# Row maxima of a causal attention kernel: diagonal pairs first, with half of their masking moved to ScalarE and GpSimd

## The chip, the cores and the metric

The kernel runs on one core of a Trainium2 chip. The metric is the device time of one execution in microseconds. Of the five engines four compute: TensorE (PE in the profile; its weight loads are PEld), VectorE (DVE), ScalarE (ACT) and GpSimd (POOL). SyncE (SP) issues most DMAs. Each engine takes its own instructions in the order in which the program lists them, and waits on semaphores for the others.

## What is computed

One transformer block in float32 on 4096 tokens of 256 features: causal attention with 16 heads of 16 features, and then a feed-forward network. Only the attention matters here.

```python
h = layernorm(x)
q, k, v = split(h @ w_attn + b_attn)            # 16 heads of 16 features
logits = einsum('bhqd,bhkd->bhqk', q, k) * hd ** -0.5
logits = where(causal, logits, -inf)
weights = softmax(logits, axis=-1)
out = einsum('bhqk,bhkd->bhqd', weights, v) @ w_proj + b_proj
x = x + layernorm(out)
...                                              # the feed-forward network
```

The softmax needs the maximum of each row of the logits (one query, one head, all keys up to the query). The kernel computes all logits twice: once with queries on the partitions, to find the maxima, and once with keys on the partitions, to take the exponential and to multiply by v.

## The kernel before

**Tiling.** Queries come in 8 blocks j of 512, heads in 4 groups g of four. An *item* is one (j, g); there are 32, worked off in the order of j, then g. Keys come in chunks c of 512, and because the attention is causal block j needs the chunks 0 to j. Tiles of 128 queries in a block are t = 0 to 3.

**Steps.** Item (j, g) has 4(j+1) steps kt, each of 128 keys. In a step the loop at line 946 does, in the order of the program:
- the first half of a *pair* of the maxima (`MaxUnit`, lines 612 to 687): the logits of 128 queries against one chunk of 512 keys, for heads 2 and 3 of the group (`pr` is 1), two matmuls into two PSUM banks of the three-bank pool `pm` (L624);
- the scores of this step for heads 0 and 1, then 2 and 3 (`ScoreUnit`, L729): eight matmuls, two of which per bank subtract the row maximum by a product with `ones`; then ScalarE's exponential (L744);
- the second half of the pair (heads 0 and 1, `pr` is 0);
- the values of an earlier step (L779), and pieces of background work: `prep` of the block j+2 (normalization, transposition `pt`, projections `pk`, `pq`, `pv`) and `project` of the block j-1 (`py`), whose GpSimd parts are additions, normalizations and casts.

In the last four steps of an item (kt of 4j to 4j+3) the keys are those of the diagonal chunk. There the scores and values have 512, 384, 256 and 128 columns only, and GpSimd sets the upper triangle of one 128x128 block per head to zero (`affine_select` on e, L749).

**The maxima.** They run ahead of the scores by an item and three pairs (`LEAD`): during item n the loop issues the pairs of item n+1 from its fourth on, and in the last three steps the first three pairs of item n+2. `maxima` (line 600) lists the pairs of an item: for each t the chunks 0 to j, so that each t ends with its diagonal pair, which has (t+1)*128 columns. `MaxUnit.finish` reduces them on VectorE:
- a full pair's head: one `tensor_reduce` of 512 columns (L658). In most steps ScalarE first copies one of the first two heads from PSUM to SBUF (`hold`, L643), and VectorE reduces the copy afterwards (L647); `lent` lists other work of ScalarE that takes this copy's place, and in the last three steps there is none;
- a diagonal pair's head: one masked operation (`tensor_tensor_reduce`, L662) that adds a mask of 0 and -1e30 and takes the maximum, followed by a read of its accumulator;
- after the diagonal pair of t, a small reduction over the chunks into `neg` (L675), and after the last t three small operations that split `neg` into a rounded part and its rest in `mcol` (L681 to L686).

`to_rows` (line 689) turns `mcol` into a row with four matmuls (`pmt`, L694) and a copy on ScalarE (`mrow`, L703), at the end of the next step. The scores of the item need `mrow`.

**What sets the order.** Everything in this part is issued by hand in the order of the loop (`manual_schedule`). The planner is the arithmetic at lines 945 to 952: `due` is the number of pairs of this step. A block's items have as many steps as the next item has pairs, save the last one, whose successor has four more. Up to four extra pairs of a block are issued between the matmuls of the background (`unit_beside`, line 884, in the items g = 0 to 2). The keys of an item come by DMA into a ring of 16 tiles per pair of heads (`keys`, `ask`).

**The start.** `prep` of the blocks 0 and 1 runs first (lines 908 to 915; that of block 1 has its casts on GpSimd), then seven pairs of maxima, then `to_rows` of the first item (lines 916 to 920).

Of the kernel before, what the change touches and what calls it, by code (L numbers as in the profile page):

```python
# [24 lines left out]
LEAD = 3  # L25

# [67 lines left out]
def sandwich_kernel(  # L94
# [131 lines left out]
    for key, at in (("h1", 0), ("h2", FC)):  # L226
        TAGS[key] = {(c, o): f"k{at + c}_{o}" for o in range(2) for c in range(FC)}
# [142 lines left out]
    xT0 = []  # L370


    with ExitStack() as actx:
# [137 lines left out]
        chunks = [(n, c) for n in range(G * NB) for c in range(n // G + 1)]  # L511
        RING = 2 * NB
        kT, asked = {}, [0]

        def keys(n, c):

            for pr in range(2):
                kT[n, c, pr] = load_rows(
                    f"k{asked[0] % RING}_{pr}", f"k{n}_{c}_{pr}", "k", c, 4 * (n % G) + 2 * pr
                )  # L520
            asked[0] += 1

        def ask(n, kt):

            while asked[0] < len(chunks) and chunks[asked[0]][0] <= n + 2:

                if asked[0] >= RING and chunks[asked[0] - RING] >= (n, (kt - 1) // NT):
                    return
                if n >= 2 * G and kt % 2:
                    return  # L530
                keys(*chunks[asked[0]])
                if n >= 2 * G:
                    return
# [66 lines left out]
        def maxima(j, g):  # L600

            mcol = mcols[g % 2]
            neg = stat.tile([P, NT, 4], F32, tag="neg", name=f"neg_{j}_{g}")
            for t in range(NT):
                mx = stat.tile([P, 4, NB], F32, tag="mx", name=f"mx_{j}_{g}_{t}")
                for c in range(j + 1):
                    n = QB if c < j else (t + 1) * P
                    yield [(j, g, t, c, pr, n, mx, neg, mcol) for pr in (1, 0)]  # L610

        class MaxUnit:
            def __init__(self, j, g, t, c, pr, n, mx, neg, mcol):
                self.at = j, g, t, c, pr
                self.n, self.mx, self.neg, self.mcol = n, mx, neg, mcol
                self.ps = {h: bank(f"pm_{j}_{g}_{t}_{c}_{h}") for h in (2 * pr, 2 * pr + 1)}
                self.diagonal = c == j

            def products(self):
                j, g, t, c, pr = self.at  # L620
                n = self.n
                for i, ps in enumerate(self.ps.values()):
                    r = slice(i * P // 2, (i + 1) * P // 2)
                    nc.tensor.matmul(  # L624
                        ps[:, 0:n],
                        lhsT=qT[j, g][pr][r, t * P : (t + 1) * P],
                        rhs=kT[G * j + g, c, pr][r, 0:n],
                        start=True,
                        stop=True,
                    )  # L630

            def finish(self, hold=False):
                j, g, t, c, pr = self.at
                n = self.n
                heads = list(self.ps.items())
                if hold:


                    h, ps = heads.pop(0)
                    held = const.tile(  # L640
                        [P, QB], F32, tag=f"xT0{'hl'[c % 2]}", name=f"held_{j}_{g}_{t}_{c}"
                    )
                    nc.scalar.copy(held[:, 0:n], ps[:, 0:n])  # L643
                    heads.append((h, held))
                for h, ps in heads:
                    if not self.diagonal and hold and ps is held:
                        nc.vector.tensor_scalar(  # L647
                            held[:, 0:n],
                            held[:, 0:n],
                            -3.0e38,  # L650
                            None,
                            ALU.max,
                            ALU.max,
                            accum_out=self.mx[:, h, c : c + 1],
                        )
                        continue
                    if not self.diagonal:
                        nc.vector.tensor_reduce(  # L658
                            self.mx[:, h, c : c + 1], ps[:, 0:n], AX.X, ALU.max
                        )  # L660
                        continue
                    nc.vector.tensor_tensor_reduce(  # L662
                        out=ps[:, 0:n],
                        in0=ps[:, 0:n],
                        in1=mask[:, QB - n : QB],
                        scale=1.0,
                        scalar=-3.0e38,
                        op0=ALU.add,
                        op1=ALU.max,
                        accum_out=self.mx[:, h, c : c + 1],  # L670
                    )
                if not (self.diagonal and pr == 0):
                    return False
                neg, mcol = self.neg, self.mcol
                nc.vector.tensor_reduce(  # L675
                    neg[:, t, :], self.mx[:, :, 0 : j + 1], AX.X, ALU.max, negate=True
                )
                if t < NT - 1:
                    return False
# [3 lines left out]
                col = mcol.rearrange("p t (i pr e) -> p t pr i e", i=2, pr=2)  # L683
# [3 lines left out]
                return True  # L687
# [108 lines left out]
        mcols = [aw.tile([P, NT, P], F32R, tag=f"mcol{i}", name=f"mcol{i}") for i in range(2)]  # L796
        for mcol in mcols:
            nc.gpsimd.memset(mcol.bitcast(F32), 0.0)
# [70 lines left out]

        def issue(unit, **how):  # L870
            unit.products()
            done = unit.finish(**how)
            if done is True:
                rows_due.append((now + 4, unit))
            return done
# [9 lines left out]
        def unit_beside():  # L885
            j, g = item
            if not begun_pair and 1 <= j < NB - 1 and g < G - 1 and len(ahead) < NT:
# [28 lines left out]
        while issued < first[1] + LEAD:  # L916
            for args in next(stream):
                issue(MaxUnit(*args))
            issued += 1
        rows_of(now + 4)  # L920
        for n, (j, g) in enumerate(items):
# [15 lines left out]
            if (j, g) == (NB - 1, G - 1):  # L937
                W["h1"] = weight_pieces("h1", TAGS["h1"])
                load_pieces(rounded["h1"], W["h1"])
            item = j, g  # L940
            if g == G - 1:
                issued += len(ahead)
                ahead.clear()
            begun = issued
            goal = min(first[min(n + 2, len(items))] + LEAD, first[-1])
            for kt in range(count[n]):
# [3 lines left out]
                due = begun + (goal - begun) * (kt + 1) // count[n] - issued  # L950
                pairs = [next(stream) for _ in range(due)]
                issued += due
                es = []
                if pairs:
                    unit = MaxUnit(*pairs[0][0])
                    issue(unit, hold=not (lent or xT0) and unit.n > QB // 2 and kt <= NT * j)
                    lent.clear()
                es = [
                    issue(ScoreUnit(j, g, kt, pr, not pairs and next(alone)))
                    for pr in range(2)  # L960
                ]
                if pairs:
                    issue(MaxUnit(*pairs[0][1]))
                values.step(now + 1)
# [11 lines left out]
                if j > 0 and kt % 4 == 2 and kt < NT * j:  # L976
                    next(halving, None)
            rows_of(now + 2)
# [255 lines left out]
```

## Time and profile before

| What | Value |
|---|---|
| Time, median of 3 runs | 2401.88 us (2397.31 to 2404.38) |
| The profiled execution: time, span | 2401.19 us, 2399.5 us |
| Its mean granted TensorE clock | 0.982 |
| From the start to the first steps (0 to 80 us) | VectorE busy 24.92 us, clock 0.82 |
| Block 0 (80 to 153 us) | VectorE busy 45.81 us of 73, clock 0.78 |
| Blocks 1 to 7 while there are maxima (153 to 1667 us) | PE busy 1484.77, VectorE 1346.93, ScalarE 1246.95, GpSimd 464.84 us of 1514 |
| Last item (1667 to 1736 us) | PE busy 68.68, ScalarE 61.51 us of 69 |
| Feed-forward network (1736 to 2399.5 us) | PE busy 653.57 us of 663.5 |

How to read the profile: times are in microseconds unless marked ns, and L624 is line 624 of the kernel. A group of instructions has its line, engine, operation, output and inputs, count, busy time, mean duration in ns, and the engine's idle time before it with what ended it. A matmul's end is modelled, and its duration is more than its share of the stream, so a busy PE need not be a PE at its peak. The chain of waits is followed back from the last instruction: at each step to what released it, or to the instruction before it on the same engine.

### The profile page before, as it was taken

Reading aid. Unit: us, or ns where it says so; the run is one execution under the profiler, and the core shown is the slowest. Engines: PE = TensorE matmul, PEld = TensorE weight load, DVE = VectorE, ACT = ScalarE, POOL = GpSimd, SP = SyncE. Lnnn points to the kernel's source line nnn. Section 1 sums busy time; section 2 is a strip of 40 time slices with the busy share of each in tenths; the row PEclk is TensorE's granted clock in tenths of the full one; section 3 lists DMA queues with packets and bytes.
Section 4 is the critical chain, followed back from the end, with each engine's and each line's share of the span. In section 5 each row is a group of like instructions: output and inputs, shape, how many; then the busy total and the mean of one; then the engine's idle time right before and its main releaser. Section 6 shows DMA issues by size and latency. Waiting matters only on the chain.

```text
span 2399.5 us, 40893 instructions
## 1 busy us (share of the span) xinstructions
PE 2318.1 (97%) x15237; PEld 1408.6 (59%) x15237; DVE 1768.1 (74%) x4102; ACT 1514.3 (63%) x2087; POOL 565.9 (24%) x898
## 2 busy tenths in 40 slices
PE   4889999999999999999999999999999999999998
PEld 2545554455554555545555555544488888888887
DVE  1667887998999899988999998986056546544653
ACT  1447787887797888888899888976822222222221
POOL 2324334432334223243223321010002100000000
PEclk8879999999999999999999999999999999999999
DMA  4443534433332432244323232111021000000000
GB/s 144 159 151 123 176 101 159 138 115 106 112 97 96 145 123 75 97 159 120 111 77 96 81 115 62 54 54 62 7 97 46 27 1 18 18 18 1 18 9 11
DMA packets 134831, 202.78 MB, mean 85 GB/s; under 512 B 14912, under 2 KB 59584, under 8 KB 134624
## 3 DMA queue, kind: packets, MB, share of 16 engines
q1 hardware_dynamic: 132672, 198.75, 25.4%
q8 instruction: 122, 2.00, 0.4%
q10 hardware_dynamic: 1776, 1.18, 0.2%
q14 instruction: 85, 0.70, 0.1%
q0 software_dynamic: 176, 0.15, 0.1%
HBM read 137.91 MB, written 62.13 MB: 83 GB/s over the span
## 4 chain that ended last, share of the span: by engine, by line
PE 87%; DVE 6%; ACT 2%; DMA 2%; POOL 1%; issue 1%; SPq 0%; ACTq 0%; POOLq 0%; DVEq 0%
PE av L779 21%; PE s L729 19%; PE z L1090 19%; PE pm L624 15%; PE pyf L1172 2%; PE za L1090 2%; PE zb L1090 2%; DVE mx L658 2%; DVE pm L662 2%; PE py L280 1%; PE pk L465 1%; PE pv L586 1%; PE pq L465 1%; PE pmt L694 1%; ACT e L744 1%
## 5 line engine op out<-in xcount | busy, mean ns | idle before, releaser
L744 ACT ACTIVATE e<-s 128x1024 f32<-128x1024 f32 (+3 forms) x1175 | 1039.7, 936 | 101.0 <-PE s L729 90.5
L658 DVE TENSOR_REDUCE mx<-pm 128x1 f32<-128x512 f32 x1496 | 963.1, 685 | 132.1 <-PE pm L624 90.8
L624 PEld LDWEIGHTS pm<-k,q 64*128 64x128 f32 x2304 | 301.2, 186 | 498.6 <-DVE mx L658 344.4
L624 PE MATMUL pm<-k,q 64*128 64x512 f32 (+3 forms) x2304 | 569.8, 439 | 22.8 <-DVE mx L658 11.7
L779 PE MATMUL av<-e,v 128*32 128x512 f32 (+3 forms) x4608 | 580.3, 575 | 0.6 <-POOL e L749 0.6
L729 PE MATMUL s<-q,k 64*128 64x512 f32 (+3 forms) x2304 | 465.2, 389 | 9.6 <-ACT e L744 2.0
L729 PE MATMUL s<-mrow,ones 64*128 64x512 f32 (+3 forms) x2304 | 452.6, 379 | 0.0
L1157 ACT ACTIVATE fb<-z,sh 128x512 f32<-128x512 f32 x128 | 88.3, 690 | 364.8 <-PE z L1090 339.5
L729 PEld LDWEIGHTS s<-q,k 64*128 64x128 f32 x2304 | 230.6, 187 | 79.8 <-issue 17.8
L662 DVE CUSTOM_DVE_ANT_0 pm<-pm,mask 128x128 f32<-128x128 f32 (+3 forms) x463 | 212.6, 499 | 73.1 <-PE pm L624 68.1
L749 POOL TENSOR_SCALAR_AFFINE_SELECT e<-e 128x256 f32<-128x256 f32 x256 | 103.0, 411 | 682.4 <-ACT e L744 680.7
L729 PEld LDWEIGHTS s<-mrow,ones 64*128 64x128 f32 x2304 | 234.3, 187 | 37.1 <-ACT mrow L703 0.5
L643 ACT COPY held<-pm 128x512 f32<-128x512 f32 (+1 forms) x345 | 200.2, 580 | 50.2 <-PE pm L624 17.7
L647 DVE TENSOR_SCALAR_CACHE_REDUCE held<-held 128x512 f32<-128x512 f32 x296 | 200.1, 676 | 0.1
L1090 PE MATMUL z<-hb_0h,h 128*128 128x512 f32 x512 | 199.3, 389 | 0.0
L1090 PE MATMUL z<-hb_0l,h 128*128 128x512 f32 x512 | 199.2, 389 | 0.0
L779 PEld LDWEIGHTS av<-e,v 128*32 128x32 f32 x4608 | 91.6, 108 | 145.5 <-issue 129.0
L202 POOL TENSOR_TENSOR rstd<-ve,neghalf 128x4 f32<-128x4 f32 (+1 forms) x22 | 20.8, 945 | 632.9 <-DVE ve L200 607.4
L1057 DVE CAST hb_1h<-fb 128x512 fp32r<-128x512 f32 x64 | 27.3, 427 | 156.0 <-ACT fb L1157 156.0
L1134 ACT ACTIVATE sl<-za,s 128x512 f32<-128x512 f32 x64 | 44.0, 690 | 120.0 <-PE za L1090 58.2
L1090 PEld LDWEIGHTS z<-hb_0l,h 128*128 128x128 f32 x512 | 96.1, 188 | 19.9
L1090 PEld LDWEIGHTS z<-hb_0h,h 128*128 128x128 f32 x512 | 96.1, 188 | 19.9
(251 smaller groups left out, 2553.6 us busy)
## 6 DMA issues: line engine op xcount, KB each, us to landing
k<-k SPq DMA_DIRECT2D x288, 256.0 KB
q<-q SPq DMA_DIRECT2D x64, 256.0 KB
x<-in_x_dram SPq DMA_DIRECT2D x16, 512.0 KB
k<-hik SPq DMA_DIRECT2D x32, 256.0 KB
k<-lok SPq DMA_DIRECT2D x32, 256.0 KB
q<-hiq SPq DMA_DIRECT2D x32, 256.0 KB
q<-loq SPq DMA_DIRECT2D x32, 256.0 KB
avd<-av_sb SPq DMA_DIRECT2D x32, 256.0 KB
```

The costliest lines, as they stand in the source:

```text
L465: nc.tensor.matmul(ps, lhsT=wqk[d][:, i * D + c * P : i * D + (c + 1) * P], rhs=xTs[j][:, d, :], start=(d == 0), stop=(d == DC - 1),)
L624: nc.tensor.matmul(ps[:, 0:n], lhsT=qT[j, g][pr][r, t * P : (t + 1) * P], rhs=kT[G * j + g, c, pr][r, 0:n], start=True, stop=True,)
L643: nc.scalar.copy(held[:, 0:n], ps[:, 0:n])
L647: nc.vector.tensor_scalar(held[:, 0:n], held[:, 0:n], -3.0e38, None, ALU.max, ALU.max, accum_out=self.mx[:, h, c : c + 1],)
L658: nc.vector.tensor_reduce(self.mx[:, h, c : c + 1], ps[:, 0:n], AX.X, ALU.max)
L662: nc.vector.tensor_tensor_reduce(out=ps[:, 0:n], in0=ps[:, 0:n], in1=mask[:, QB - n : QB], scale=1.0, scalar=-3.0e38, op0=ALU.add, op1=ALU ...
L729: nc.tensor.matmul(self.ps[i][:, self.q0 :], lhsT=(self.k, ones[pr])[m][r, :], rhs=(qT[j, g][pr], mT[j, g])[m][r, self.q0 :], start=(m == ...
L744: nc.scalar.activation(e[:, at : at + n, q0:], ps[:, :, q0:], AF.Exp)
L749: nc.gpsimd.affine_select(out=at, in_=at, compare_op=ALU.is_ge, fill=0.0, base=0, pattern=[[0, 2], [1, P]], channel_multiplier=-1,)
L779: nc.tensor.matmul(self.av[h * HW : (h + 1) * HW, q0:], lhsT=vb[kt // NT][:, kt % NT, o : o + HW], rhs=es[h // 2][:, h % 2, q0:], start=(k ...
L1090: nc.tensor.matmul(ps, lhsT=w[c], rhs=single(part[:, c, :]), start=(c == 0 and i == 0), stop=(c == kc - 1 and i == parts - 1),)
L1157: nc.scalar.activation(h, z, AF.Gelu, scale=sc[:, oc : oc + 1])
```

## The change

- `maxima` lists the four diagonal pairs of an item first, for t = 2, 1, 0, 3, and then the full pairs. With the lead of three pairs, the diagonal pairs t = 2, 1, 0 of item n+2 come in the last three steps of item n, and t = 3 in the first step of the next.
- For heads 2 and 3 of a diagonal pair ScalarE copies the last 128 columns of each head (the block on the diagonal) to SBUF, GpSimd masks the two blocks in one `affine_select`, and VectorE reduces the columns before them with plain reductions (none for t = 0) and the two masked blocks with one reduction, which is put off (`owed`) until `pay`: right after the first half of the pair in the loop, and after both halves in the seven pairs of the start. Heads 0 and 1 keep the masked operation on VectorE.
- The maxima of all t of an item lie in one tile `mx`, with a column more, which GpSimd fills with -1e30 at the item's beginning; one small reduction per item replaces four. It and the operations on `mcol` (now a single tile) are put off in the same way (`end_group`).
- The held copies use fixed tiles (`spares`). The scores' second matmuls come before the second half of the pair and their exponential after it. `to_rows` is due 2 instead of 4 counts of `now` after the (now later) end of the group.
- In blocks 1 to 5 each step has one pair; extra pairs are issued beside the background in the items g = 2 and 3 alone, and what is left in the last step. Block 6 has none beside the background.
- A ring place of the keys comes free when its chunk's scores are done (`homes`, `free`), in the new order of the chunks. The weights h1 and h2 take their tiles accordingly.

```diff
-        chunks = [(n, c) for n in range(G * NB) for c in range(n // G + 1)]
+        chunks = [(n, c) for n in range(G * NB) for c in (n // G, *range(n // G))]
...
+            mx = stat.tile([P, NT, 4, NB + 1], F32, tag="mx", bufs=2, name=f"mx_{j}_{g}")
+            nc.gpsimd.memset(mx[:, :, :, j + 1 : j + 2], NEG)
+            for t in (2, 1, 0, 3):
+                yield [(j, g, t, j, pr, t * P, mx, False) for pr in (1, 0)]
             for t in range(NT):
-                mx = stat.tile([P, 4, NB], F32, tag="mx", name=f"mx_{j}_{g}_{t}")
-                for c in range(j + 1):
-                    n = QB if c < j else (t + 1) * P
-                    yield [(j, g, t, c, pr, n, mx, neg, mcol) for pr in (1, 0)]
+                for c in range(j):
+                    yield [(j, g, t, c, pr, QB, mx, (t, c) == (NT - 1, j - 1)) for pr in (1, 0)]
...
+                if self.diagonal and pr == 1:
+                    edge = spares[t % 2][:, 1, 0 : 2 * P].rearrange("p (h q) -> p h q", h=2)
+                    if len(owed) > 1:
+                        owed.popleft()()
+                    for i in range(2):
+                        nc.scalar.copy(edge[:, i, :], self.ps[i][:, n : n + P])
+                    if n:
+                        for i in range(2):
+                            nc.vector.tensor_reduce(
+                                self.mx[:, t, 2 + i, j + 1 : j + 2], self.ps[i][:, 0:n], AX.X, ALU.max)
+                    nc.gpsimd.affine_select(
+                        out=edge, in_=edge, compare_op=ALU.is_ge, fill=NEG,
+                        base=0, pattern=[[0, 2], [-1, P]], channel_multiplier=1)
+                    owed.append(
+                        lambda: nc.vector.tensor_reduce(self.mx[:, t, 2:4, j], edge, AX.X, ALU.max))
+                    return
...
-            if not begun_pair and 1 <= j < NB - 1 and g < G - 1 and len(ahead) < NT:
+            if not begun_pair and 1 <= j < NB - 2 and g >= G - 2 and len(ahead) < NT:
...
+                if 1 <= j < NB - 2:
+                    due = 1
+                    if (g, kt) == (G - 1, count[n] - 1):
+                        due = goal - issued - len(ahead)
...
                     unit = MaxUnit(*pairs[0][0])
-                    issue(unit, hold=not (lent or xT0) and unit.n > QB // 2 and kt <= NT * j)
+                    issue(unit, hold=not (lent or xT0) and kt <= NT * j)
                     lent.clear()
-                es = [
-                    issue(ScoreUnit(j, g, kt, pr, not pairs and next(alone)))
-                    for pr in range(2)
-                ]
+                pay()
+                es = [issue(ScoreUnit(j, g, kt, 0, not pairs and next(alone)))]
+                unit = ScoreUnit(j, g, kt, 1, not pairs and next(alone))
+                unit.products()
                 if pairs:
                     issue(MaxUnit(*pairs[0][1]))
+                es.append(unit.finish())
```

## The prediction

> **What bounds the kernel now.** I read the page's first lines, then its chain of waits, and then the chain and the busy times inside one item. All numbers are of the profiled execution: span 2399.5 us, time 2401.19 us, 0.7 us under the median of 2401.88. A difference below 0.3% (7.2 us) cannot be told from none here.
>
> ```profile
> span 2399.5 us, 40893 instructions
> PE 2318.1 (97%) x15237; PEld 1408.6 (59%) x15237; DVE 1768.1 (74%) x4102; ACT 1514.3 (63%) x2087; POOL 565.9 (24%) x898
> ...
> PE 87%; DVE 6%; ACT 2%; DMA 2%; POOL 1%; issue 1%; SPq 0%; ACTq 0%; POOLq 0%; DVEq 0%
> ```
>
> TensorE carries 87% of the chain and VectorE 6%, about 144 us. Where those 6% lie decides. The chain in order of time inside item (6,1) gives a ruler: each "PE s" starts a step (one kt).
>
> ```profile
> 1197.51 0.93 PE s L729 x8
> ...
> 1200.10 0.93 PE s L729 x8
> ...
> 1202.57 0.92 PE s L729 x8
> ...
> 1205.04 0.93 PE s L729 x8
> ```
>
> An ordinary step takes 2.59 us. In the chain it is TensorE alone: first score pair of the maxima 0.43, scores 0.93, second pair 0.24, values 1.00. The two steps from 1200.10 hold the diagonal pair t=1 (256 columns instead of 512) and take 2.47 each. So **inside an item a diagonal pair is cheaper than a full one**: 0.24 us over two steps for t=1, by the same view 0.12 for t=2 and nothing for t=3; for t=0 I take 0.24, as t=1. VectorE gains nothing there. The end of the item is another matter (busy times by step; kt 21 and 22, then 25 to 27, then kt 0 and 1 of the next item):
>
> ```profile
> 1236.06:1238.65 2.59, 2.59 (x23) 1.34 (x22) 2.49 (x5) 2.47 (x3) 0.00 (x0) 1.00 0.00 0
> 1238.65:1241.26 2.61, 2.61 (x23) 1.37 (x22) 2.54 (x8) 2.47 (x3) 0.00 (x0) 1.00 0.00 0
> ...
> 1247.14:1249.84 2.70, 2.70 (x25) 1.34 (x24) 2.48 (x4) 2.22 (x5) 1.11 (x3) 1.00 0.00 0
> 1249.84:1252.33 2.49, 2.41 (x25) 1.18 (x24) 2.45 (x4) 2.42 (x9) 0.82 (x2) 1.00 0.00 0
> 1252.33:1254.59 2.26, 2.15 (x22) 1.17 (x21) 2.25 (x5) 1.08 (x4) 1.22 (x4) 1.00 0.43 142
> 1254.59:1256.97 2.38, 2.16 (x24) 1.39 (x22) 2.38 (x6) 2.19 (x3) 2.19 (x4) 1.00 0.87 292
> 1256.97:1259.80 2.83, 2.83 (x25) 1.47 (x27) 1.81 (x11) 2.83 (x5) 2.66 (x5) 1.00 0.46 143
> ```
>
> Columns: length; busy PE, PEld, DVE, ACT, POOL; clock; DMA. In the three diagonal steps of the scores (384, 256, 128 columns) VectorE is busy 2.25 to 2.48 us with four full reductions, while TensorE and ScalarE have less to do: VectorE binds. This is where the change puts the small diagonal pairs.
>
> **The prices.**
>
> By form, VectorE, ScalarE and GpSimd (count | busy us, mean ns of one | idle before):
>
> ```profile
> L658 DVE TENSOR_REDUCE mx<-pm 128x1 f32<-128x512 f32 x1496 | 963.1, 685 | 132.1 <-PE pm L624 90.8 <-PE s L729 19.2
> ...
> L662 DVE DVE_READ_ACCUMULATOR2_ANT mx<- 128x1 f32 x512 | 69.5, 136 | 0.0
> ```
>
> ```profile
> L643 ACT COPY held<-pm 128x512 f32<-128x512 f32 x322 | 189.1, 587 | 48.7 <-PE pm L624 17.7
> ```
>
> ```profile
> L749 POOL TENSOR_SCALAR_AFFINE_SELECT e<-e 128x256 f32<-128x256 f32 x256 | 103.0, 411 | 682.4 <-ACT e L744 680.7
> ```
>
> Rows of the timeline start 0.60 us apart for a plain reduction of 512 columns, and 0.65, 0.515, 0.38 and 0.25 for masked ones of 512, 384, 256 and 128 with their accumulator read. A plain one of 128, 256 or 384 columns has no row; between [128x4] (159 ns) and 512 (685 ns) on a line, started 80 ns apart less, I take 0.20, 0.34 and 0.47. A copy of 128 columns on ScalarE lies on the line of 384 and 512 (481, 587 ns) at 0.27. The mask has the shape of L749: 0.41, and it starts 0.07 after ScalarE ends.
>
> VectorE's work for a diagonal pair falls to 2.05 (t=2), 1.5, 0.85 and 2.6 us (t=3), where four reductions of a full pair take 2.41. Over the program the second pair's masked operations (half of 315.7 us: L662's forms on pm 212.6, on held blocks 33.6, their reads 69.5) become 192 plain reductions (80.6) and 128 of the blocks (about 52.7 at the 412 ns of a [128x256] reduction in SBUF); 96 small neg operations go (13); 78 more pairs with a held half cost 6. **About 30 us less on VectorE.** ScalarE gets 256 small copies (69 us) and 52 more full ones (30) for 23 of 384 less (11): +88. POOL gets 128 masks (53) and 32 fills. TensorE's matmuls stay the same in number and shape.
>
> **The new wait.** VectorE's queue in a diagonal step is: rests, block reduction, masked A', masked B' (the pair's other heads). In the built program the rests wait for ScalarE's copy of the same bank, and the block reduction waits for POOL's mask. Behind it stands A', and for A' waits TensorE: the three pm banks let the next step's first pair start only 0.13 us after A' ends (in the timeline a reduction ends at 1232.79 and the matmul starts at 1232.92). From the end T of the step's first matmuls: copies done T+0.5, masked T+0.98, block reduction from T+1.04.
> - t=0 (kt 27): no rest covers the wait: block until 1.38, A' 1.63, then 0.13 and a matmul of 0.5: **2.25** (now 2.26).
> - t=1 (kt 26): the copies come 0.15 later behind the mrow copy; block until 1.47, A' 1.85, matmul 0.3: **2.30** (now 2.49).
> - t=2 (kt 25): rests and the group's end (0.57) cover the wait; A' ends at 2.62: **3.15**, with the 0.59 of pmt inside (now 2.70 without).
> - t=3 (kt 0): rests from 0.38 to 1.32, block 1.66, A' 2.31: **2.93** (now 2.38).
> - kt 1: ScalarE's copy of av, which made it 2.83, fits into the longer kt 0: **2.60**.
>
> Full pairs in kt 21 to 24 take 2.59 each, now 2.59, 2.61, 3.18 (with pmt) and 2.70. The nine windows go from 23.74 to 23.59 (-0.15), the diagonal pairs that leave the body cost 0.6: **+0.45 for an item, +12 us for the 26 items of blocks 1 to 7 that have such an end.**
>
> [...]
>
> **The other terms.**
> - Ends of items with background work (about 20). Two stretches:
>
> ```profile
> 1479.40:1491.90 12.50, 11.86 (x83) 7.20 (x81) 7.88 (x18) 6.18 (x14) 5.12 (x9) 1.00 0.08 21
> 647.40:662.10 14.70, 13.64 (x92) 7.43 (x88) 12.59 (x32) 7.19 (x20) 4.60 (x7) 1.00 0.06 20
> ```
>
> The first has no pair beside the projection, and VectorE is busy 7.9 of 12.5 us: nothing to gain. The second has two more, 1.1 us each, and VectorE 12.6 of 14.7. The change takes 2.8 us off VectorE in each. Gain between 0 and 1.1 an end; I take 0.5, nearer the first because POOL's 1.28 us additions and 1.27 us casts stand ahead of masks: **-10** (0 to -22).
> - Masks at kt 0 queued behind POOL's background work (six in the built order, 1.9 to 3.8 us): **+3** (0 to +12).
> - Block 6 places two pairs in ordinary steps instead of beside the projection, 2.16 against 1.1 each: **+2**.
> - The start. POOL's last cast of the second block stands ahead of the first fill of mx and the first mask:
>
> ```profile
> 72.00 1.27 POOL L484 TENSOR_TENSOR loq<-fullq,hiq 128x512 fp32r<-128x512 f32 x1 [2.85 <-DMA k<-lok]
> ```
>
> VectorE starts its first masked operation at 65.58 now, and could start only after 73.3; seven pairs (12 us) then put pmt at about 85 instead of 78.5. The short steps of block 0's first items may give 2 back: **+4.5** (0 to +9).
> - Fewer, later extra pairs (g of 2 and 3 instead of 0 to 2) and the keys' new order move no work that the chain shows: 0. Scores' second products before the max unit change no engine's order: 0.
>
> Sum: 12 - 10 + 3 + 2 + 4.5 = +11.5. **2401.2 + 11.5 = 2412.7, about 2412**; the median of before stands 0.7 above the execution that I reckon from.
>
> **The rivals.**
> - **Balance wins (faster).** Place: the three last steps of an item. If masks and copies run ahead of VectorE, because it is still busy with the step before, nothing waits. VectorE's content there falls by 2.8 us an item, 73 us in 26 items; were the block ready at once, t=0 and t=1 gain 0.4 to 0.6 each: 26 us. With that, and 0.5 more in each background end (-10): 2412 - 36 = 2376; three quarters of it, 2385, is my figure. It decides from the point where the wait before block reductions is under about 0.2 us on average. For it: ScalarE is busy only 1.08 of 2.26 us in kt 27. Against: the copy, mask and two hand-overs are 0.98 us in sequence, and t=0 has nothing to cover them.
> - **POOL blocks (much slower).** 23 of the masks of t=1 and t=0 and the six at kt 0 stand behind 1.3 to 3.8 us of background; if all were paid in full, +25 and no gain at background ends: about 2440. Against: TensorE has 1.7 us of projection at the same time.
> - **Nothing.** TensorE's chain covers all but the start: 2405. The change would then do on VectorE what it says and no step would move.
>
> **How the numbers follow.** My case 0.50 (of it 0.32 slower, 0.17 within 0.3%, 0.01 faster); balance 0.30 (0.28 faster, 0.02 within); POOL 0.14 (slower); nothing 0.06 (0.04 within, 0.02 slower). Faster 0.29, same 0.23, slower 0.48. Range: 2380 (background ends at -22, half of the covered waits) to 2432 (masks at kt 0 at +12, background ends at 0); my case alone holds 2396 to 2424.
>
> **What would show it.** Right: block reductions on VectorE wait for POOL, longest for t=0; kt 0 of an item near 2.9 us; kt 25 to 27 near 3.15, 2.3, 2.25; the first pmt near 85; VectorE's busy time near 1740 (1768 - 30), ScalarE's near 1600 (1514 + 88). Wrong: no wait there and kt 26 and 27 under 2 us (balance), or waits over 1 us behind L299 and L484 (POOL). I would also be wrong if TensorE's ordinary step left 2.59.

## The result, and the profile after

The median went from 2402.77 us (4 runs) to 2472.11 us (4 runs, 2469.44 to 2478.94): a ratio of 1.0297 (95% interval 1.0269 to 1.0325). The change makes the kernel 69 us slower. The direction was forecast, the size was not: 2412 us, in a range that ended at 2432.

The profiled execution took 2474.22 us. From its page, the span, the busy times and the chain of waits (shares by engine):

```profile
span 2472.4 us, 41474 instructions
...
PE 2358.7 (95%) x15237; PEld 1433.7 (58%) x15237; DVE 1741.2 (70%) x3892; ACT 1577.5 (64%) x2372; POOL 613.9 (25%) x1057
...
PE 80%; issue 6%; DVE 4%; ACT 4%; DMA 2%; POOL 2%; SPq 0%; ACTq 0%; POOLq 0%; DVEq 0%
```

VectorE has lost 27 us of work, as meant. TensorE has the same 15237 matmuls and is busy 41 us longer. The mean granted clock fits that: 0.965 after, 0.982 before. I count clock lost as span times (1 - clock): 86.5 us after, 43.2 before (means over all executions on record: 82 after, 43 before). Of the 73 us by which the span grew, 41 are thus TensorE's longer busy time and 32 its longer idle time.

Where the time is, by the starts of the scores of each step in the two traces (73 us in all; the feed-forward part adds 0.5):

| Stretch | After minus before |
|---|---|
| Start, to the first scores | +6.3 us |
| Block 0 | +4.7 |
| Blocks 1 to 7: last three steps of the items | +43.0 |
| ... of these, nine ends with the features `pk`, `pq` of `prep` in them | +37.1 |
| ... seven ends with the projection `py` in them | -6.3 |
| ... the others | +12.2 |
| Blocks 1 to 7: the first two steps of the items | +19.8 |
| All other steps | -1.4 |

The waits after (who, for whom: us in total, times, longest). In the new kernel L610 fills the spare column of `mx`, L656 copies the blocks, L659 reduces the columns before them, L665 masks, L675 reduces the masked blocks:

```profile
DVE mx L659 <- ACT sparel L656: 79.0, 55, 5.9
...
DVE mx L675 <- POOL spareh L665: 69.4, 27, 5.8
...
DVE mx L659 <- POOL mx L610: 54.8, 21, 28.7
PEld pm L631 <- DVE mx L659: 52.7, 65, 7.0
...
PE pm L631 <- DVE mx L659: 28.6, 35, 6.7
```

Three hand-overs hold VectorE, and TensorE waits behind it for a bank. Counted from the first scores on, both names of each tile together: 63 waits for copies make 86 us (31 of them over 1 us), 55 for masks 87 us (34 over 1 us), 20 for the fill 26 us. Meanwhile ScalarE ran the row statistics of the background (27 us), the copies (24) and `mrow` (7); GpSimd ran the masks (18), the casts of the features (18) and additions `y` (12). These 200 us are waits of VectorE, not time of the kernel: TensorE's idle time grew by the 32 us above.

Item (6,1), in which the prediction was worked out, shows it. Stretches from kt 24 on: length, busy PE, PEld, DVE, ACT, POOL, clock, DMA.

```profile
1302.46:1304.99 2.53, 2.53 (x22) 1.27 (x22) 2.43 (x6) 2.41 (x4) 0.41 (x1) 1.00 0.02 6
1304.99:1308.36 3.37, 3.22 (x26) 1.80 (x26) 2.78 (x11) 2.18 (x6) 1.70 (x5) 1.00 0.00 0
1308.36:1312.55 4.19, 3.17 (x22) 1.29 (x24) 1.99 (x9) 4.09 (x14) 1.23 (x3) 0.77 0.00 0
1312.55:1315.35 2.80, 2.80 (x22) 1.86 (x24) 0.93 (x5) 1.52 (x6) 1.74 (x5) 0.50 0.38 119
1315.35:1319.01 3.66, 3.09 (x21) 1.65 (x17) 2.08 (x6) 2.85 (x5) 3.38 (x6) 0.72 0.67 195
```

In kt 26 (4.19 us) ScalarE is busy 4.09 us and VectorE 1.99: VectorE waits for ScalarE. ScalarE's timeline there:

```profile
1308.32 0.59 ACT L736 CAST mrow<-pmt 128x512 fp32r<-128x512 f32 x1 [1.12 <-PE pmt L727]
1308.80 0.51 ACT L181 ACTIVATE junk<-y,mvy 128x256 f32<-128x256 f32 x1
1309.21 0.19 ACT L181 ACTIVATION_READ_ACCUMULATOR junk<-y,mvy 128x1 f32 x1
1309.44 0.42 ACT L173 ACTIVATE junk<-y 128x256 f32<-128x256 f32 x1
1309.76 0.19 ACT L173 ACTIVATION_READ_ACCUMULATOR junk<-y 128x1 f32 x1
1309.85 0.41 ACT L656 COPY sparel<-pm 128x128 f32<-128x128 f32 x2
```

The products of t=1 were issued at 1308.21, their copies start at 1309.85, behind `mrow` and 1.1 us of statistics. VectorE waited 1.47 us for them:

```profile
1310.13 0.49 DVE L659 TENSOR_REDUCE mx<-pm 128x1 f32<-128x128 f32 x2 [1.47 <-ACT sparel L656]
```

From 1310.6 on the clock is 0.50, for 6.8 us (the last section shows these stretches).

Beside the features it is worse (six of the nine ends lose 3.1 to 8.7 us each), and through GpSimd. The chain of waits in the end of item (5,2) (start, us):

```profile
1078.31 0.70 ACT fullk L474
1079.01 0.06 issue
1079.07 0.62 POOL hik L482
...
1080.99 0.42 POOL spareh L665
1081.41 0.02 issue
1081.44 0.42 DVE mx L675
1081.86 0.20 DVE pm L682
1082.06 0.07 DVE mx L682
1082.13 0.04 issue
1082.17 0.79 PE pm L631
```

The mask waits behind two casts (L482 and L484) until 1080.99, VectorE waits 3.40 us for it and TensorE 1.35 us for VectorE; from 1081.9 on the clock is halved for 6.8 us. From the timeline:

```profile
1079.77 1.27 POOL L484 TENSOR_TENSOR lok<-fullk,hik 128x512 fp32r<-128x512 f32 x1
...
1081.44 0.42 DVE L675 TENSOR_REDUCE mx<-spareh 128x2 f32<-128x256 f32 x1 [3.40 <-POOL spareh L665]
...
1082.17 0.79 PE L631 MATMUL pm<-k,q 64*128 64x512 f32 x1 [1.35 <-DVE mx L682]
```

### The profile page after: what moved, and what is told of

Its sections match the earlier page's. It is cut to its first block, busy times and chain, and to the rows that moved or that the text cites. A ratio compares the mean times of both kernels' runs of the same rounds, so it can differ in the third digit from the quotient of the medians.

```text
span 2472.4 us, 41474 instructions
## 1 busy us (share of the span) xinstructions
PE 2358.7 (95%) x15237; PEld 1433.7 (58%) x15237; DVE 1741.2 (70%) x3892; ACT 1577.5 (64%) x2372; POOL 613.9 (25%) x1057
## 4 chain that ended last, share of the span: by engine, by line
PE 80%; issue 6%; DVE 4%; ACT 4%; DMA 2%; POOL 2%; SPq 0%; ACTq 0%; POOLq 0%; DVEq 0%
PE av L812 19%; PE s L762 18%; PE z L1140 17%; PE pm L631 15%; PE za L1140 2%; PE zb L1140 2%; PE pyf L1222 2%; ACT e L777 2%; PE pk L465 1%; DVE mx L659 1%; PE pv L591 1%; PE pq L465 1%; PE pmt L727 1%; PE py L279 1%; DVE pm L682 1%
## 5 line engine op out<-in xcount | busy, mean ns | idle before, releaser
L631 PE MATMUL pm<-k,q 64*128 64x512 f32 (+3 forms) x2304 | 595.9, 447 | 55.3 <-DVE mx L659 28.6
L631 PEld LDWEIGHTS pm<-k,q 64*128 64x128 f32 x2304 | 317.6, 190 | 559.3 <-DVE mx L700 364.6
L762 PE MATMUL s<-q,k 64*128 64x512 f32 (+3 forms) x2304 | 474.9, 392 | 9.7 <-ACT xT L580 1.9
L762 PE MATMUL s<-mrow,ones 64*128 64x512 f32 (+3 forms) x2304 | 463.1, 384 | 0.0
L762 PEld LDWEIGHTS s<-q,k 64*128 64x128 f32 x2304 | 240.2, 191 | 71.5 <-issue 17.8
L762 PEld LDWEIGHTS s<-mrow,ones 64*128 64x128 f32 x2304 | 244.5, 190 | 41.7 <-ACT mrow L736 0.5
L659 DVE TENSOR_REDUCE mx<-pm 128x1 f32<-128x256 f32 (+2 forms) x192 | 73.5, 419 | 142.0 <-ACT sparel L656 79.0
L698 ACT COPY spareh<-pm 128x512 f32<-128x512 f32 x203 | 119.2, 587 | 30.9 <-PE pm L631 6.4
L703 DVE TENSOR_SCALAR_CACHE_REDUCE spareh<-spareh 128x512 f32<-128x512 f32 x203 | 137.2, 676 | 0.0
L682 DVE CUSTOM_DVE_ANT_0 pm<-pm,mask 128x384 f32<-128x384 f32 (+3 forms) x256 | 120.5, 510 | 14.8 <-PE pm L631 14.6
```

The costliest lines, as they stand in the source:

```text
L631: nc.tensor.matmul(self.ps[i][:, 0:n], lhsT=qT[j, g][pr][r, t * P : (t + 1) * P], rhs=kT[G * j + g, c, pr][r, 0:n], start=True, stop=True,)
L659: nc.vector.tensor_reduce(self.mx[:, t, 2 + i, j + 1 : j + 2], self.ps[i][:, 0:n], AX.X, ALU.max,)
L682: nc.vector.tensor_tensor_reduce(out=ps[:, 0 : n + P], in0=ps[:, 0 : n + P], in1=mask[:, QB - n - P : QB], scale=1.0, scalar=-3.0e38, op0= ...
L698: nc.scalar.copy(held, self.ps[0])
L703: nc.vector.tensor_scalar(held, held, -3.0e38, None, ALU.max, ALU.max, accum_out=best[0])
L762: nc.tensor.matmul(self.ps[i][:, self.q0 :], lhsT=(self.k, ones[pr])[m][r, :], rhs=(qT[j, g][pr], mT[j, g])[m][r, self.q0 :], start=(m == ...
```

## The experiments

All seventeen start from the changed kernel; "before" ran beside each. The kernels of 7 and 8 start from vector_masks, which has no split. Times are medians, with the ratio to before and its 95% interval.

**1. Take the wait for the mask away** (late_pay). Result: 2466.5 us, ratio 1.026 (1.0233 to 1.0287).

```diff
-edge = spares[t % 2][:, 1, 0 : 2 * P]
-if len(owed) > 1:
-    owed.popleft()()
+at = t // 2 * 2 * P
+edge = spares[t % 2][:, 1, at : at + 2 * P]
...
-owed.append(lambda: nc.vector.tensor_reduce(self.mx[:, t, 2:4, j], edge, AX.X, ALU.max))
+owed.append((now + 4, lambda: nc.vector.tensor_reduce(self.mx[:, t, 2:4, j], edge, AX.X, ALU.max)))
...
-while owed:
-    owed.popleft()()
+while any(at <= now for at, _ in owed):
+    owed.popleft()[1]()
```

> The changed kernel, but the reduction of the masked blocks is issued two steps later on VectorE (four block tiles in place of two); all work and all else stays. Theory A, held queue: the 71 us come from VectorE standing in its own order before the block reductions, because GpSimd's masks stand behind casts and additions; TensorE then idles over 1 us and its clock is halved after that (87 us of clock lost in the trace after, 44 before, counted as half of each stretch at half clock). With the wait for the mask gone, about half of the loss in the item ends goes: near 2435 us, waits for the mask (now 69 us) under 10 us, and fewer stretches at half clock than the 23 of now. Rival B, crowding: the extra pairs now lie beside the projections of the items g of 2 and 3 and make these ends long whoever masks: 2465 to 2475. Rival C, ScalarE: the copies, behind ScalarE's row statistics, are what VectorE waits for (79 us in the trace after): 2455 to 2465.

VectorE has no wait for masks left in the list, but VectorE's waits for copies of `sparel` grow from 79.0 to 108.3 us. Only 6 us came back (the intervals overlap), a time in rival B's range, while the longer waits for copies are rival C's: the mask is not the half that theory A took it for.

**2. Reductions ahead of the copies, too** (late_rests). 2459.3 us, 1.0237 (1.022 to 1.0254).

```diff
-for i in range(2):
-    nc.scalar.copy(edge[:, i, :], self.ps[i][:, n : n + P])
 if n:
     for i in range(2):
         nc.vector.tensor_reduce(...)
+for i in range(2):
+    nc.scalar.copy(edge[:, i, :], self.ps[i][:, n : n + P])
```

> As late_pay, and in the program the plain reductions of the columns before the block come ahead of ScalarE's copies, so that they need not wait for the copies of the same bank (the copies wait for them). Theory A with both legs (mask and copy): 2405 to 2425 us, and VectorE waits for ScalarE's copies under 20 us in all (now 79). Theory A with the mask alone: as late_pay, within 5 us. Rival B, crowding: 2465 to 2475. Rival C, ScalarE: the gain comes here and not in late_pay, 2415 to 2430.

Missed again. VectorE no longer waits for ScalarE, but the copies now free the banks, and TensorE waits for them (waits of late_rests, where L664 is the copy):

```profile
PEld pm L632 <- ACT spareh L664: 44.3, 38, 7.6
...
PE pm L632 <- ACT spareh L664: 33.5, 35, 7.3
```

**3. No split** (vector_masks). 2397.9 us, 0.9979 (0.9968 to 0.999).

```diff
-if self.diagonal and pr == 1:
+if self.diagonal and False:
...
-accum_out=self.mx[:, t, i, j : j + 1],
+accum_out=self.mx[:, t, 2 * pr + i, j : j + 1],
```

> The changed kernel's order and placing of the pairs, but VectorE masks heads 2 and 3 of the diagonal pairs itself with the masked operation, as it does heads 0 and 1; no copies of blocks, no masks on GpSimd. Theory A: no chain over three engines is left, so the item ends come back to their lengths of before although VectorE has some 30 us more to do: 2395 to 2412 us, clock near 0.98, at most 11 stretches at half clock. Rival B, crowding: the order alone is to blame, 2450 or more. Rival D, the late end of the group (the row of maxima now comes in the item's end): 2425 to 2440.

As theory A had it, but for one stretch at half clock: the profiled execution, the slowest of the eight, has 12, and at most 11 were written. The split costs 74 us (2472.1 - 2397.9); all the rest of the change together gains about 5. The first scores are back at 80.9 us. The last three steps of the items, where the changed kernel loses 43.0 us, take 9.6 us less than before. But the nine ends with the features take 16.7 us more even here, so 16.7 of their 37.1 us are the placing's and not the split's. The split itself costs 20.4 us in these nine ends, 13.3 in the seven with the projection and 18.8 in the twelve others: it is dear at every kind of end.

**4. Extra pairs placed as before, with and without the split** (beside_early, vm_beside). 2443.8 us, 1.0164 (1.0147 to 1.0181); 2385.5 us, 0.9934 (0.9918 to 0.9951).

```diff
-if not begun_pair and 1 <= j < NB - 2 and g >= G - 2 and len(ahead) < NT:
+if not begun_pair and 1 <= j < NB - 1 and g < G - 1 and len(ahead) < NT:
...
-if 1 <= j < NB - 2:
-    due = 1
...
-elif (j, g, kt) == (NB - 2, G - 2, count[n] - 1):
-    due += 1
...
```

> The changed kernel with the copies and masks, but the extra pairs of a block are placed as before (beside the background of the items g of 0 to 2, and the same count of pairs per step). Theory A: diagonal pairs still meet GpSimd's and ScalarE's background in the item ends, only in other items: 2435 to 2465 us. Rival B, crowding: the seven ends with projections that lost 45 us come back: 2420 to 2430, and of the rest the start keeps 6 us and block 0 5 us.

> Order of the pairs as in the changed kernel, VectorE masks all heads, extra pairs placed as before. With the split, the old placing was 28 us better than the new one. If the placing costs by itself (crowding), it is better here too: 2375 to 2385. If the placing costs only through the split (it puts diagonal pairs among the projections' work, where copies and masks queue), it is no better here: 2395 to 2410.

beside_early lies in theory A's range. (The ends that its rival B calls "seven ends with projections that lost 45 us" are the nine with the features of the table above, 37.1 us. With the old placing they lose nothing, and the seven with the projection lose 10.8.) The new placing costs 28 us with the split and 12 without it: crowding is real, and smaller than the split; vm_beside's 2385.5 lies half a us above the range written for crowding. **vm_beside beats both kernels, by 16 us against before.** Against before its last three steps of all items take 20.4 us less, its other steps and the start 5 more.

```profile
span 2383.7 us, 40948 instructions
...
PE 2312.0 (97%) x15237; PEld 1410.9 (59%) x15237; DVE 1753.1 (74%) x4062; ACT 1519.7 (64%) x2094; POOL 564.8 (24%) x929
...
PE 89%; DVE 3%; ACT 2%; issue 2%; DMA 2%; SPq 1%; POOL 1%; ACTq 0%; POOLq 0%; DVEq 0%
```

VectorE's share of the chain is 3% where it was 6%, though it has 12 us more work than in the changed kernel. That is still 15 us less than in before, as vm_beside keeps more of the change than the order of the pairs: one small reduction per item in place of four, the later scores, the fixed tiles. What each of these gains alone was not run.

**5. The three hand-overs one by one.** In these seven kernels the fill, the copy or the mask is given to VectorE. Core edits:

```diff
-nc.gpsimd.memset(mx[:, :, :, j + 1 : j + 2], NEG)
+nc.vector.memset(mx[:, :, :, j + 1 : j + 2], NEG)
...
-nc.scalar.copy(edge[:, i, :], self.ps[i][:, n : n + P])
+nc.vector.tensor_copy(edge[:, i, :], self.ps[i][:, n : n + P])
...
-nc.gpsimd.affine_select(out=edge, in_=edge, ...)
-owed.append(lambda: nc.vector.tensor_reduce(self.mx[:, t, 2:4, j], edge, AX.X, ALU.max))
+owed.append(masked)
```

`masked` is one masked operation per block on `edge`; in fill_only and apart_only it works on the block in PSUM at once, with no copy.

| Kernel | Hand-overs left | us | over vector_masks |
|---|---|---|---|
| vector_masks | none, one masked operation per head | 2397.9 | |
| apart_only | none, columns and block apart | 2421.4 | +23 |
| fill_only | fill | 2449.9 | +52 |
| copy_alone | copy | 2461.2 | +63 |
| own_fill | copy, mask | 2461.6 | +64 |
| mask_alone | mask (VectorE copies) | 2464.8 | +67 |
| mask_only | fill, mask (VectorE copies) | 2467.9 | +70 |
| after | fill, copy, mask | 2472.1 | +74 |
| copy_only | fill, copy | 2476.3 | +78 |

> The changed kernel without GpSimd's part: ScalarE still copies the diagonal blocks of heads 2 and 3, VectorE masks and reduces the two copies (two masked operations of 128 columns) where it reduced them after the mask. With VectorE masking everything in place the time was 2398 us, with both legs 2472. Theory A1, the copy is the costly leg (VectorE and the pm banks wait for copies that stand behind ScalarE's statistics, projections' copies and exponentials): 2440 to 2460. Theory A2, the mask is the costly leg: 2400 to 2415.

> The changed kernel without ScalarE's part: VectorE copies the two blocks, GpSimd masks them, VectorE reduces them. Theory A1, the copy on ScalarE is the costly leg: 2405 to 2425 (VectorE has more to do and still waits for masks). Theory A2, the mask on GpSimd: 2440 to 2465. If the legs only add up, copy_only's and mask_only's losses against 2398 sum to 74; if either alone makes the others wait, they sum to more.

> The changed kernel, with the fill of the spare column of mx on VectorE in place of GpSimd. VectorE's first reduction of columns in an item now waits for the fill, which stands behind GpSimd's casts at the start and behind its masks and additions in the items (26 us of waits in the items, and the first scores 6 us late). If the three hand-overs (fill, copy, mask) add up: the start gets its 5 to 6 us back and the items some 10 more: 2455 to 2460. If one of them alone is enough to hold VectorE, as copy_only and mask_only suggest: the start's 5 to 6 us alone, about 2466. If the start is late for another reason: 2470 or more.

> The changed kernel without ScalarE's copies and GpSimd's masks: VectorE reduces the columns before the block and masks the block in two operations each, both in PSUM; of the hand-overs GpSimd's fill alone stays. VectorE has 192 more operations than with the masked operation on all columns (about 40 us of busy time). If the fill alone is enough to hold VectorE: 2450 to 2470. If not: vector_masks (2398) plus the late start (6 us) plus 5 to 15 for the fill in the items and the additional operations: 2409 to 2425.

> fill_only with the fill on VectorE: VectorE reduces the columns before the block and masks the block in operations of their own, and no other engine takes part. If the fill's waits made fill_only's 52 us: back to 2400 to 2412 us, first scores at 81. If the additional operations on VectorE (192, where VectorE binds in the item ends) made them: 2430 to 2445.

> copy_only (2476 us) with the fill on VectorE: ScalarE's copies are the only hand-over. If the copy alone holds VectorE in most item ends: 2455 to 2470. If it was the fill together with the copy: 2420 to 2440.

> mask_only (2468 us) with the fill on VectorE: GpSimd's masks are the only hand-over, and VectorE makes the copies. If the mask alone holds VectorE in most item ends: 2450 to 2465. If it was the fill together with the mask: 2415 to 2435.

Only copy_alone and mask_alone fall in a range written for them, both times the one in which a single hand-over is enough. copy_only and mask_only came out above both of their ranges, fill_only at the lower edge of its first, own_fill just above the range for adding up, and apart_only between its two.

Two things were not expected. First, doing columns and block apart costs 23 us by itself, though VectorE's busy time grows by only 11 (1759.7 to 1770.7): the step of t=2 in item (6,1) takes 3.69 us where vector_masks takes 3.16. Second, over apart_only each hand-over alone brings 29 (fill), 40 (copy) and 43 us (mask, with VectorE's copies and 25 us more work of VectorE in it), 112 in sum, and all three together 51. So none of the three is *the* cause; I read it as waits that cover each other in VectorE's order, which is argued, not shown. The late start comes from GpSimd's queue, by the fill as by the mask: the first scores stand at 80.9 us in copy_alone, at 88.1 in fill_only and 88.4 in mask_alone.

**6. The best that order can do for the split** (split_best: the edits of 1, 2, 4 and the fill on VectorE). 2417.1 us, 1.0067 (1.0051 to 1.0084).

> All that spares VectorE a wait with the split kept: extra pairs placed as before, fill on VectorE, reductions of columns ahead of the copies, reductions of the masked blocks two steps later. Against vm_beside (2385 us), the same without the split, it tells whether the split can be saved by a better order. If the waits on VectorE are all there is: 2380 to 2395, since VectorE has less to do than with its own masks. If banks held by ScalarE's copies take the place of these waits: 2410 to 2435.

32 us above vm_beside, in the range written for banks that ScalarE's copies hold. The trace bears out a part of that: TensorE waits 15 us for these copies (10.3 and 5.1 us for its two tiles). Another part may be what columns and block apart cost without any hand-over, 23 us in 5; that was not run with the old placing. None of the orders tried saves the split.

**7. What a delay of VectorE costs** (stall_2, stall_6). 2404.0 us, 1.0016 (1.0006 to 1.0026); 2479.4 us, 1.0316 (1.028 to 1.0351). The edit of stall_6; stall_2 has 2 in place of 6:

```diff
-for i, ps in enumerate(self.ps):
+again = 6 if (pr, t) == (0, 1) and j > 0 else 0
+for i, ps in enumerate([self.ps[0]] * again + self.ps):
+    i = max(i - again, 0)
```

> vector_masks (2398 us), and VectorE repeats the masked operation of one head of the diagonal pair t=1 six times in the blocks 1 to 7: a delay of six times 0.38 us, 2.3 us, once in each of 28 items, and no other work. It measures what a delay of VectorE in the item end costs, and what the clock adds. If a delay costs its own length and no more: +64 us, 2462, and clock lost stays near the 53 us of vector_masks. If a stall of TensorE of over about 1 us halves its clock for 3.4 us or twice that: 15 to 28 more stretches at half clock, 25 to 75 us more clock lost, 2485 to 2530 us. If VectorE's slack there hides the delay: under 2430.

> As stall_6, with two repeats in place of six: a delay of VectorE of 0.76 us in each of 28 items. stall_6 cost 81 us for 64 us of delay, with 46 us more clock lost. If the clock falls in proportion: a third of 81, 27 us, 2425. If there is a threshold, and 0.76 us of delay leaves TensorE busy enough: clock lost as in vector_masks (53) and 10 to 21 us more time, 2408 to 2419. If the item ends have slack for it: 2398 to 2405.

The delays were longer than written. Here are repeats of one head in stall_6 (the first two, then the head's own operation and the other head's, which works on the other bank):

```profile
1308.78 0.43 DVE L684 CUSTOM_DVE_ANT_0 pm<-pm,mask 128x256 f32<-128x256 f32 x1
...
1309.31 0.43 DVE L684 CUSTOM_DVE_ANT_0 pm<-pm,mask 128x256 f32<-128x256 f32 x1
...
1311.93 0.43 DVE L684 CUSTOM_DVE_ANT_0 pm<-pm,mask 128x256 f32<-128x256 f32 x1
...
1312.28 0.47 DVE L684 CUSTOM_DVE_ANT_0 pm<-pm,mask 128x256 f32<-128x256 f32 x1
```

Here a repeat on the same bank starts 0.525 us after the one before (3.15 us for six); the other head's operation, on the other bank, starts 0.35 us after (0.35 in before too, from 1202.61 to 1202.96), near the 0.38 written. So six repeats delay VectorE by 3.15 us and two, by the same distance, by 1.05, in each of 28 items.

stall_2 costs 6 us for 29 us of delay, 0.2 an item: the item end has some 0.8 us of slack. stall_6 costs 81 us for 88, 2.9 an item, a little less than the delay's own length. Its time lies between the ranges written, and by the longer delay the one for "its own length" would have been 2486 and not 2462. From stall_2 to stall_6, though, 59 us more delay cost 75 us more time (give or take 9), 1.3 for one. That in a fixed order of work a delay by itself pushes the end back by no more than its length is my reasoning, which no run shows; by it something else costs about 17 us there. The clock is the candidate, since 47 us more of it are lost (means over all executions: 44 in stall_2, 92 in stall_6); that it is the clock is argued.

**8. Fill the stall with useless products** (stall_6_filled, filled). 2472.3 us, 1.029 (1.027 to 1.031); 2417.2 us, 1.0057 (1.0036 to 1.0079).

```diff
+if second.diagonal and second.at[0] > 0 and second.at[2] == 1:
...
+    filler = two_banks(f"filler_{jj}_{gg}")
+    for k in range(6):
...
+        nc.tensor.matmul(filler[:, k % 2, :], lhsT=qT[jj, gg][0][r, 0:P], rhs=kT[G * jj + gg, jj, 0][r, :], start=True, stop=True)
```

> stall_6 (2479 us, 99 us of clock lost), and after the second half of the diagonal pair t=1 TensorE makes six useless products of 512 columns (1.3 us by the 0.43 us that two of them take in the chain of before), in a spare pair of banks; they come just ahead of the place where TensorE waits for VectorE. Theory A, the clock is a cost of its own: the products fill the stall, the clock is lost less (60 to 75 us) and more work gives a shorter time: 2445 to 2468 us. If the loss of clock only goes along with the stall and costs nothing by itself: 2479 or more, up to 2479 plus 33 us (26 times 1.3) where the products are not covered.

> vector_masks (2398 us) with the same useless products and no stall. They should cost what they take where TensorE is the bound: up to 26 times 1.3, 33 us, 2431; less where TensorE had idle time in that step (the step after t=1 takes 2.3 to 2.5 us with less than that of work): 2405 to 2425. It is the control: were it under 2398, the products would help without any stall.

By themselves the products (23 items) cost 19 us; in the stall they cost nothing, and the clock lost falls from 97 to 74 us (92 to 73 by the means of all executions). But the gain of 7 us is less than expected, the time lies between the two ranges written, and the intervals of stall_6 and stall_6_filled overlap: the sign agrees with the clock as a cost of its own, the size is not settled by this pair.

Another measure: executions of one program differ in how much clock they lose. Over 127 executions (45 of before, 82 of the other 18 kernels), each taken from its kernel's own mean, the span rises by 0.49 us for each us of clock lost (standard error 0.03, correlation 0.83). This is a correlation, and a longer wait may raise both. Read as a price, it makes 19 us of lost time out of the 40 us more that the changed kernel loses on average; the growth of TensorE's busy time, 41 us, would allow all of them.

## Why the prediction was wrong, step by step

- **The step that failed** is in "The new wait": "From the end T of the step's first matmuls: copies done T+0.5, masked T+0.98, block reduction from T+1.04." It took ScalarE's and GpSimd's queues as empty. With it the last three steps were to take 0.25 us more in each of 26 items, and with the -10 us for ends with background work some 3 us less in all; they took 43.0 us more, and 9.6 us less than before when VectorE did all masks. The stretches quoted there had ScalarE busy 2.42 of 2.49 us in kt 26 itself; the statistics in it came to stand before the copies. Predicted against measured in item (6,1) for kt 25, 26, 27, 0 and 1: 3.15, 2.30, 2.25, 2.93, 2.60 against 3.37, 4.19, 2.80, 3.66, 2.95 us. With VectorE doing all masks: 3.16, 2.05, 2.41, 2.27, 2.95. The sign "block reductions wait for POOL, longest for t=0" did come: 69.4 of the 87 us are t=0's, 27 waits of 2.6 us on average.
- **No term for the clock.** Each stall was priced at its length. About 40 us more clock was lost; between 0 and all of that is lost time, and what runs 7 and 8 show speaks for a part.
- "Fewer, later extra pairs ... 0": 28 us with the split, 12 without. They brought more pairs into the ends with the features. Nine such ends cost 37 us, of which 16.7 remain when VectorE does all masks; the masks behind the features' casts, as in item (5,2), come on top.
- "Ends of items with background work: -10": near for the seven ends with the projection (-6.3), but by luck: with VectorE doing all masks they gain 19.6, and the split took 13.3 back. Wrong for those with features.
- "Masks at kt 0 ... +3 (0 to +12)": with the 0.32 us an item that its sum gives kt 0 and 1 (8 us in 26 items) the first two steps were to cost 11 us (8 to 20). They cost 19.8, near the upper end; 8.1 us of it remain when VectorE does all masks.
- The fill was counted at the start alone. In the items it makes 26 us of waits.
- "The start ... +4.5" was 6.5 for the start and -2 for block 0. The start came out right: +6.3, with the first pmt at 84.9 for 85. Block 0 gave nothing back: +4.7. Block 6: its middle steps take 2.6 us more, for +2.
- Busy times: VectorE 1741.2 for 1740; ScalarE 1577.5 for 1600, in part because two copies of a pair overlap (0.41 us for both in kt 26, 57.1 us for all 256, not 0.54 and 69). Right, and of no use: VectorE's work was not what the wait depended on.
- The wait for ScalarE's copy of the same bank, which the prediction has end at T+0.5, is the largest of the three kinds together with the mask's (86 and 87 us of VectorE's waits). late_rests turned it round, and TensorE waited instead.
- The rival "POOL blocks" was named at 0.14 and 2440 us: half of the mechanism, without ScalarE's queue and without the clock. 34 of the 55 waits for masks were over 1 us, the sign written for it. "Balance wins" was right about the place, the last three steps: vm_beside gains 20.4 us there, without the split. Its point of decision, a wait before block reductions under 0.2 us, was met with the split in late_pay, and the gain did not come: the waits for copies grew instead.
- Two sums do not come out of the terms that they name: the lower end of the range, 2380 (2412.7 - 12 - 13 is 2388), and the rival at "about 2440" (2401.2 + 12 + 25 + 2 + 4.5 is 2445). The miss does not hang on either.

## What to carry to other kernels

When the engine that binds is to hand work to others and take it back, price the hand-over with what stands in their queues at that moment, not with the operations' own durations: 27 us less work on VectorE came with some 200 us of waits. Try the new order and the new split apart: here the change without the split, and with the old placing, gained 16 us, and the split lost 74 us in the new placing, 58 in the old and 32 in the best order tried. And do not scale a measured delay: 1.05 us in each item cost 0.2 us, 3.15 us cost 2.9.

## What the runs showed of the clock

In the trace after, TensorE did not stand still before its clock fell. Between 200 and 1740 us its granted clock is 0.50 in 16 stretches: seven of 3.41 us, seven of 6.83 and two of 10.24. All of them begin on one grid of 3.41 us. Five stretches of that grid in item (6,1) to (6,2), columns as above:

```profile
1303.78:1307.19 3.41, 3.26 (x30) 1.50 (x28) 2.82 (x10) 3.35 (x6) 1.71 (x5) 1.00 0.02 5
1307.19:1310.61 3.42, 2.40 (x24) 1.49 (x16) 1.95 (x9) 2.26 (x9) 0.69 (x2) 1.00 0.00 0
1310.61:1314.02 3.41, 3.41 (x25) 1.83 (x29) 1.42 (x7) 3.24 (x12) 1.60 (x5) 0.50 0.00 0
1314.02:1317.43 3.41, 3.41 (x20) 1.82 (x14) 1.74 (x7) 1.49 (x4) 2.97 (x6) 0.50 0.88 248
1317.43:1320.85 3.42, 2.77 (x26) 1.53 (x28) 2.90 (x8) 2.22 (x4) 3.25 (x7) 1.00 0.49 161
```

In the second TensorE is busy 2.40 of 3.42 us, idle for 1.02; the next two run at half clock (0.50). Of the 16 beginnings (before had 2 between 200 and 1740 us) 15 follow a stretch of the grid in which TensorE was busy 56 to 74%, and one follows a stretch of 98%. Seven stretches no busier than those 15 were not followed by one, so in this trace the share of busy time alone does not tell when the clock falls.
